# Two graph layers on one core: the last block's values laid out by tokens, its weighted sums formed by quarters

## The chip, the core and the metric

The kernel runs on one core of a Trainium2 chip. The core has five engines that work side by side and wait for each other by semaphores: TensorE (PE in the profile, its weight loads PEld), VectorE (DVE), ScalarE (ACT), GpSimd (POOL) and SyncE (SP), which here only issues transfers. The metric is the time of one execution on the device, in microseconds, as the median of several.

## What is computed

The input x is 128 graphs of 64 nodes with 768 features, adj a 64 by 64 adjacency for each graph. Layer 0 (attention by the product of x with itself, three weight matrices, a normalisation, relu) gives a residual that is added to x and normalised. Layer 1 is attention with 12 heads of 64 features over the same graphs. Its end is what this change is about:

```python
q = _split_heads(input_graph @ Wq + bq)
k = _split_heads(input_graph @ Wk + bk)
v = _split_heads(input_graph @ Wv + bv)
scores = jnp.einsum('bhqd,bhkd->bhqk', q, k) / sqrt(HD)
scores = scores + beta * adj_e                      # masked where adj is 0
probs = jax.nn.softmax(scores, axis=-1)
out = jnp.einsum('bhqk,bhkd->bhqd', probs, v)
...
x = _layernorm(x + out, axis=-1)
```

All of it is in float32.

## The kernel before

**Blocks and tiles.** The 8192 tokens are taken in 16 blocks (`NBLK`) of 512 tokens, which is 8 graphs. A block has four tiles of 128 tokens (`T`), two graphs on the partitions of a tile. A loop over n works on block n's layer 1 and block n + 1's layer 0 at once. What remains of the block before (p = n - 1) is pushed into it too.

**The order of the work** is written out by hand. A weight product of a block is computed by seven products of half-size matrices (`seven`, with the order `ORDER` = 1, 2, 6, 5, 7, 4, 3). Each of the seven has two parts j, so that there are 14 units, places 0 to 13. Each unit is three matrix calls of 128 by 128 by 384, which the profile shows as six records. Before a unit, `hooks` for its place are called. They put other work into PE's order. After a unit, `step()` takes the next pieces from three queues of prepared functions: `first`, `urgent` and `lazy`. Their tags (`act`, `root`, `after`, `gap`, `tiny`, `free`) say when a piece may be taken. `settle(key)` runs the queues until all pieces of that key are issued, and `freed()` empties `first`. The order of issue on an engine is the order in which it works.

**Values.** `values(n)` forms v with `by_tokens("v", ...)` through `seven`. A first product is evicted from PSUM with its bias into `u` (L415), and a later one, added to that, into `v`. For m and h as the halves of tokens and columns, the second product finishes (0, 0), the seventh (1, 1), the fourth (1, 0) and the third (0, 1). In all blocks but the last, v is evicted as one instruction of 128x384 (L774) and is then rearranged by three ACT copies (L786, L787). In the last block (`in_place`) each eviction is four instructions of 64x192 (L779), which write v into the rearranged places straight away.

**Scores.** `scores(n, hg)` works on one of three head groups (hg = 0, 1, 2) of four heads each. PE forms the scores, DVE multiplies by the mask (L839), adds (L860), takes the maximum (L861) and subtracts it (L862). ACT takes 16 exponentials of 32x256, each from one set of 32 partitions to another (L853), and DVE turns 32 by 32 squares in place (L857). The result is `eT`, exponentials with the key node on the partitions.

**Weighted sums.** `weighted(n, hg, halves)` multiplies `eT` with v and a column of ones, so that the sum of the exponentials comes out beside the sums. It does this for a head group and for a half of the tokens, with calls of 64 by 64 by 65. `added` takes the reciprocal of the sums (L888) and then adds the product to the residual tile in four scaled additions of 128x64 (L892).

**The last normalisation.** `finish_by_act` takes the sums (L937) and the squares (L940) of a tile on ACT, then the factors on DVE (L912, L915, L921, L922) with a root on ACT (L918), normalises on ACT (L926) and stores through POOL's queue (L930). `finish` takes DVE's statistics (L353, L354), a root on ACT (L361), normalises on DVE (L950) and stores through SP's queue (L951).

**The last block's end** was so ordered:

```python
values(n, {0: [partial(finish_by_act, n - 1, queue=lazy)], 4: [partial(scores, n, 2, 2, l0t)],
           12: [partial(weighted, n, 0, (1,))], 13: [partial(weighted, n, 1, (1,))]}, True)
...
weighted(n, 2, (1,))
settle(("y", n, 2))
finish_by_act(n, range(2, 4))
```

After these, the three head groups of the first half of the tokens follow, then `finish` for tiles 0 and 1. Scores of the third head group stand ahead of unit 4. Two of the six half groups of weighted sums are formed ahead of units 12 and 13, four after the last unit.

Of the kernel before, what the change touches and what calls it, by code (L numbers as in the profile page):

```python
# [51 lines left out]
def gnn_two_layers(ctx: ExitStack, tc, x, adj, wl, bl, ws, bs, wr, br, gamma, beta,  # L52
# [68 lines left out]
    def later(key, *fs, queue=lazy):  # L121
        queue.extend((key, f) if callable(f) else (key, *f) for f in fs)
# [635 lines left out]

        return one, two

    def values(n, hooks={}, in_place=False):

        def pairs(a):
            return a.rearrange("p (j r d) -> p r j d", r=2, d=HD)

        def last(t, h, ps, part):  # L770
            add = pairs(bias["v"][:, h * HALF : (h + 1) * HALF] if part is None else part)
            heads = slice(h * 3, (h + 1) * 3)
            if not in_place:
                nc.vector.tensor_tensor(v[:, t, :, heads, 0:HD], pairs(ps), add, ALU.add)  # L774
                return
            for r in range(2):
                for g in range(2):
                    rows = slice(g * L, (g + 1) * L)
                    nc.vector.tensor_tensor(v[r * L : (r + 1) * L, t, g, heads, 0:HD],  # L779
                                            pairs(ps)[rows, r], add[rows, r], ALU.add)  # L780

        by_tokens("v", blocks[n]["S"], last, None, hooks)
        if not in_place:
            low, high = v[0:L, :, 1, :, 0:HD], v[L:P, :, 0, :, 0:HD]
            swap = l0t.tile([P, T, HP, HD], F32, tag="lr", name="swap")
            later(("v", n), act(lambda: nc.scalar.copy(swap[0:L], high)), act(lambda: nc.scalar.copy(high, low)),  # L786
                  act(lambda: nc.scalar.copy(low, swap[0:L])), queue=urgent)  # L787
# [29 lines left out]
    def scores(n, hg, at_once=1, pool=None, gaps=1):  # L817

        blk = blocks[n]
        q, k = blk["qk"]
        settle("e")
# [21 lines left out]
        def exponentials(groups):  # L845
            if 0 in groups:
                blk["eT", hg] = (pool or l1e_p).tile([P, T, 2, P], F32, tag="lr" if pool else "eT", name="eT")
            e = blk["eT", hg].rearrange("p t c i -> p (t c) i")
            for a in groups:
                rows = slice(a * Q, (a + 1) * Q)  # L850
                for b in range(P // Q):
                    cols = slice(b * Q, (b + 1) * Q)
                    nc.scalar.activation(e[cols, :, rows], pairs[rows, :, cols], AF.Exp)  # L853

        def turn(h):
            e = blk["eT", hg][:, h * 2 : h * 2 + 2].rearrange("p t c i -> p (t c i)")
# [6 lines left out]
              *[act(partial(exponentials, range(a, a + at_once))) for a in range(0, P // Q, at_once)], *[GAP] * gaps,  # L863
              *([partial(turn, 0), partial(turn, 1)] if pool is None else [lambda: (turn(0), turn(1))]), queue=urgent)

    def weighted(n, hg, halves=range(2), heads=range(2)):


        blk = blocks[n]
        settle(("v", n))  # L870
        settle(("e", n, hg))
        freed()
        xt, eT = blk["x"], blk["eT", hg]
        y = {(r, h): ps_mm.tile([P, 2, 2, HD + 1], F32, tag="mm", name=f"ps_y{r}") for h in halves for r in range(2)}
        for h in halves:
            for t in range(2):
                for c in heads:
                    for r in range(2):
                        rows = slice(r * L, (r + 1) * L)
                        for g in range(2):  # L880
                            cols = slice(g * L, (g + 1) * L)
                            nc.tensor.matmul(y[r, h][cols, t, c, :], lhsT=eT[rows, 2 * h + t, c, cols],  # L882
                                             rhs=v[rows, 2 * h + t, g, hg + c * HC, :], start=True, stop=True)

        def added(h, r):
            ps = y[r, h][:, :, heads[0] : heads[-1] + 1, :]
            rz = st.tile([P, 2, 2], F32, tag="rz1", name="rz1")[:, :, 0 : len(heads)]
            nc.vector.reciprocal(rz, ps[:, :, :, HD])  # L888
            for t in range(2):
                res = xt[2 * h + t].rearrange("p (c k r d) -> p r c k d", c=2, k=HC, r=2)  # L890
                for k, c in enumerate(heads):
                    nc.vector.scalar_tensor_tensor(res[:, r, c, hg, :], ps[:, t, k, 0:HD], rz[:, t, k : k + 1],  # L892
                                                   res[:, r, c, hg, :], ALU.mult, ALU.add)

        later(("y", n, hg), *[partial(added, h, r) for h in halves for r in range(2)], queue=first)

    def finish_by_act(n, tiles=range(T), queue=urgent):

        xt, key = blocks[n]["x"], ("f", n)
        total, nm, var, std, rstd, shift = (st.tile([P, T], F32, tag=f"f{k}", name=f"f{k}") for k in range(6))  # L900
        some = slice(tiles[0], tiles[-1] + 1)

        def sums(fs):
            if queue is lazy:
                unused = l0t.tile([P, 2, D], F32, tag="lr", name="unused")[:, 0, :]
            else:
                unused = l1s_p.tile([P, T * 4 * L], F32, tag="s", name="unused")[:, 0:D]
            for t in tiles:
                fs(t, unused)

        def mean():
            nc.vector.tensor_scalar(nm[:, some], total[:, some], -1.0 / D, None, ALU.mult)  # L912

        def variance():
            nc.vector.tensor_scalar(std[:, some], var[:, some], 1.0 / D, 1e-5, ALU.mult, ALU.add)  # L915

        def root():
            nc.scalar.activation(std[:, some], std[:, some], AF.Sqrt)  # L918

        def factors():  # L920
            nc.vector.reciprocal(rstd[:, some], std[:, some])  # L921
            nc.vector.tensor_tensor(shift[:, some], nm[:, some], rstd[:, some], ALU.mult)  # L922

        def norm(ts):
            for t in ts:
                nc.scalar.activation(xt[t], xt[t], AF.Identity, bias=shift[:, t : t + 1], scale=rstd[:, t : t + 1])  # L926

        def stored(ts):
            for t in ts:
                nc.gpsimd.dma_start(out=out_t[n, t], in_=xt[t])  # L930

        def act(f):
            return f, "act" if queue is urgent else "root"

        settle(("y", n, 0))
        settle(("y", n, 1))
        later(key, (partial(sums, lambda t, o: nc.scalar.activation(o, xt[t], AF.Identity,  # L937
                                                                    accum_out=total[:, t : t + 1])), "after"),
              GAP, GAP, tiny(mean),
              act(partial(sums, lambda t, o: nc.scalar.activation(o, xt[t], AF.Square, bias=nm[:, t : t + 1],  # L940
                                                                  accum_out=var[:, t : t + 1]))),
              GAP, GAP, tiny(variance), act(root), GAP, tiny(factors),
              *[act(partial(norm, tiles[k : k + 2])) for k in range(0, len(tiles), 2)],
              (partial(stored, tiles[0:2]), "free"), GAP, GAP, (partial(stored, tiles[2:]), "free"), queue=queue)

    def finish(n, tiles=range(T)):
        xt = blocks[n]["x"]

        def norm(t, mean, rstd):
            nc.vector.tensor_scalar(xt[t], xt[t], mean, rstd, ALU.subtract, ALU.mult)  # L950
            nc.sync.dma_start(out=out_t[n, t], in_=xt[t])  # L951

        for t, mr in zip(tiles, moments(("f", n), [xt[t] for t in tiles], 1e-5, urgent)):
            later(("f", n), partial(norm, t, *mr), queue=urgent)

# [66 lines left out]
    for n in range(NBLK):  # L1024
# [20 lines left out]
        if p >= 0:  # L1045
            one = left if not last else qk[0]
            at(one, 2, scores, p, 2, *((1,) if last else (2, None, 4)))
            at(one, 5, weighted, p, 1)
            if not last and m < DEEP:
                at(left, 13, weighted, p, 2)  # L1050
                at(right, 0, finish_by_act, p)
            elif not last:
                at(right, 1, weighted, p, 2)
                at(right, 2, finish_by_act, p)
            else:
                at(qk[1], 5, weighted, p, 2)

# [92 lines left out]
        for hg in range(NHG):  # L1150
            projected(n, hg, qk[hg])

    n = NBLK - 1
    values(n, {0: [partial(finish_by_act, n - 1, queue=lazy)], 4: [partial(scores, n, 2, 2, l0t)],
               12: [partial(weighted, n, 0, (1,))], 13: [partial(weighted, n, 1, (1,))]}, True)
    settle(("f", n - 1))
    settle(("y", n, 0))
    settle(("y", n, 1))
    weighted(n, 2, (1,))
    settle(("y", n, 2))  # L1160
    finish_by_act(n, range(2, 4))
    step()
    for hg in range(NHG):
        weighted(n, hg, (0,))
        settle(("y", n, hg))
        step()
        step()
    finish(n, range(2))
    settle(("f", n))


# [29 lines left out]
```

## Time and profile before

| | |
|---|---|
| Median of three runs | 2934.7 us (2934.53 to 2936.67) |
| The profiled execution's own time | 2938.14 us |
| Span in its profile, first to last instruction | 2936.4 us |
| Mean granted TensorE clock | 0.995 |
| Busy: PE, DVE, ACT, POOL | 98%, 68%, 38%, 25% of the span |
| Values of the last block, PE's first unit | from 2881.7 us |
| PE's last unit ends | 2914.6 us |
| Last store issued by SP | 2932.3 us |

Times inside the execution count from its first instruction. A row of a timeline is its start, its duration, the engine, the line in the kernel, the operation, output and inputs by the names of the program, shapes and the number of instructions merged; in brackets, how long the engine had been idle and who ended that. A row of a group ends in total busy time, the mean of one in ns, and idle time before them. In the chain of waits each row is a start, a duration, and the instruction or wait that the end of the program hung on at that time.

### The profile page before, as it was taken

How to read it: one execution, taken by the hardware profiler on the slowest of the kernel's cores; microseconds unless marked ns; L12 is line 12 of the kernel's file. 1: busy time of each engine (PE TensorE's matmuls, PEld its weight loads, DVE VectorE, ACT ScalarE, POOL GpSimd, SP SyncE). 2: the span in 40 equal slices, each digit the busy share in tenths (PEclk: the TensorE clock that was granted, in tenths of full speed). 3: DMA queues.
4: the chain of work that ended last, by engine and by line, in shares of the span. 5: the costliest groups of instructions: out<-in, count | busy, mean ns of one | idle time of the engine just before them, and what ended most of it. 6: DMA issues, size and time to landing. Idle time of an engine off the chain costs nothing.

```text
span 2936.4 us, 49944 instructions
## 1 busy us (share of the span) xinstructions
PE 2879.9 (98%) x17578; PEld 1935.1 (66%) x17578; DVE 1989.5 (68%) x4034; ACT 1123.6 (38%) x2114; POOL 729.9 (25%) x879
## 2 busy tenths in 40 slices
PE   8999999999999999999999999999999999999997
PEld 5657567585665856658576575766757567585685
DVE  5678677676676766667667576666767667676656
ACT  0004324354243543434444344443434424354254
POOL 3133122304132130411405124051230413313110
PEclk9999999999999999999999999999999999999998
DMA  9788786849578595775958759486694966849442
GB/s 322 221 274 276 234 233 194 249 138 290 154 197 248 144 285 152 214 231 163 271 147 239 203 175 271 135 260 183 185 260 137 282 163 198 244 139 287 140 127 90
DMA packets 440278, 613.18 MB, mean 209 GB/s; under 512 B 53584, under 2 KB 416720, under 8 KB 440032
## 3 DMA queue, kind: packets, MB, share of 16 engines
q1 hardware_dynamic: 362096, 493.57, 56.0%
q10 hardware_dynamic: 60848, 44.05, 8.2%
q0 software_dynamic: 17088, 72.37, 6.7%
q8 instruction: 143, 2.34, 0.3%
q14 instruction: 103, 0.84, 0.1%
HBM read 539.43 MB, written 77.27 MB: 210 GB/s over the span
## 4 chain that ended last, share of the span: by engine, by line
PE 91%; ACT 3%; POOL 2%; DVE 2%; DMA 1%; issue 1%; SPq 0%; ACTq 0%; DVEq 0%
PE ps_X L384 35%; PE ps_Y L384 26%; PE ps_Y L638 11%; PE ps_X L638 10%; PE ps_ctx L677 3%; ACT eT L853 2%; PE sc L835 2%; PE ps_y L882 2%; PE u L527 2%; POOL q L337 1%; ACT L853 1%; ACT uqk L804 1%; POOL q L336 0%; PE ps_x L286 0%; DVE o L892 0%
## 5 line engine op out<-in xcount | busy, mean ns | idle before, releaser
L384 PE MATMUL ps_X<-xT,wqk 128*128 128x256 f32 x1728 | 395.9, 381 | 9.6 <-ACT uqk L804 9.6
L853 ACT ACTIVATE eT<-s 32x256 f32<-32x256 f32 x768 | 317.8, 414 | 184.7 <-DVE s L862 174.6
L384 PEld LDWEIGHTS ps_X<-xT,wqk 128*128 128x128 f32 x1728 | 325.8, 190 | 67.1 <-ACT uqk L804 16.2
L317 POOL TENSOR_TENSOR S<-hT 128x768 f32<-128x768 f32 x16 | 28.9, 1808 | 1133.4 <-PE ps_Y L384 1102.2
L384 PE MATMUL ps_Y<-S,wqk 128*128 128x256 f32 x1152 | 264.3, 379 | 0.0
L682 ACT ACTIVATE unused<-o 128x768 f32<-128x768 f32 x60 | 50.6, 843 | 500.4 <-DVE o L679 304.9
L384 PEld LDWEIGHTS ps_Y<-S,wqk 128*128 128x128 f32 x1152 | 218.9, 190 | 29.8
L438 DVE TENSOR_TENSOR lr<-ps_Y,u_deep 128x384 f32<-128x384 f32 x273 | 152.1, 557 | 108.6 <-PE ps_Y L638 82.8
L638 PE MATMUL ps_Y<-wlr,q 128*128 128x384 f32 x546 | 208.6, 491 | 0.0
L384 PE MATMUL ps_X<-wv,xT 128*128 128x384 f32 x576 | 195.0, 489 | 0.0
L804 ACT ACTIVATE uqk<-ps_X,bq 128x256 f32<-128x256 f32 x144 | 68.3, 474 | 324.9 <-PE ps_X L384 323.7
L812 DVE TENSOR_TENSOR q<-ps_Y,uqk 128x256 f32<-128x256 f32 x144 | 61.0, 424 | 177.7 <-ACT uqk L804 89.4
L384 PE MATMUL ps_X<-ws,hT 128*128 128x384 f32 x540 | 179.4, 486 | 0.1
L892 DVE SCALAR_TENSOR_TENSOR o<-ps_y,rz,o 128x64 f32<-128x64 f32 x768 | 165.0, 277 | 6.8
L638 PE MATMUL ps_X<-wlr,q 128*128 128x384 f32 x364 | 151.1, 497 | 14.5 <-POOL q L337 5.9
L384 PEld LDWEIGHTS ps_X<-wv,xT 128*128 128x128 f32 x576 | 108.2, 190 | 80.8 <-issue 8.4
L438 DVE TENSOR_TENSOR u_deep<-ps_X,lr 128x384 f32<-128x384 f32 x195 | 107.3, 550 | 68.0 <-PE ps_X L638 66.4
L384 PEld LDWEIGHTS ps_X<-ws,hT 128*128 128x128 f32 x540 | 102.4, 190 | 71.8 <-DMA ws<-in_L_gnn_W_self_dram 0.7
L638 PEld LDWEIGHTS ps_Y<-wlr,q 128*128 128x128 f32 x546 | 101.6, 190 | 67.2
L415 DVE TENSOR_TENSOR u<-ps_X,bv 128x384 f32<-128x384 f32 x96 | 53.4, 556 | 130.3 <-PE ps_X L384 130.2
L384 PE MATMUL ps_X<-S,wqk 128*128 128x256 f32 x576 | 138.2, 385 | 0.0
L384 PE MATMUL ps_Y<-xT,wqk 128*128 128x256 f32 x576 | 135.6, 385 | 0.0
(247 smaller groups left out, 5482.6 us busy)
## 6 DMA issues: line engine op xcount, KB each, us to landing
wlr<-lr_d SPq DMA_DIRECT2D x819, 192.0 KB, 3.5
wqk<-qk_d SPq DMA_DIRECT2D x672, 192.0 KB, 2.4
wv<-d_v SPq DMA_DIRECT2D x192, 192.0 KB, 3.3
ws<-d_s SPq DMA_DIRECT2D x180, 192.0 KB, 6.0
wv<-in_L_gnn_Wv_dram SPq DMA_DIRECT2D x144, 192.0 KB, 4.1
ws<-in_L_gnn_W_self_dram SPq DMA_DIRECT2D x135, 192.0 KB, 5.5
xa<-in_x_dram SPq DMA_DIRECT2D x64, 384.0 KB, 5.4
out_dram<-o POOLq DMA_DIRECT2D x62, 384.0 KB, 6.2
```

Source lines behind the costliest of these rows:

```text
L384: nc.tensor.matmul(ps, lhsT=a, rhs=b, start=(c == 0 and i in (1, 2, 5)), stop=(c == len(fs) - 1), skip_group_check=True)
L415: recent["u"] = evicted[nm] = nc.vector.tensor_tensor(u, ps, bias[nm][:, b * HALF : (b + 1) * HALF], ALU.add)
L438: nc.vector.tensor_tensor(dst, view(ps), add, ALU.add)
L527: nc.tensor.matmul(u[g * L : (g + 1) * L, t, :], lhsT=xT[:, c, tok], rhs=xT[:, c, tok], start=(c == 0), stop=(c == KC - 1))
L638: nc.tensor.matmul(ps, lhsT=a, rhs=b, start=(k == 0 and j in (1, 2, 5)), stop=(k == len(fs) - 1), skip_group_check=True)
L677: nc.tensor.matmul(ps[g * L : (g + 1) * L, 0:HALF], lhsT=blk["aT"][:, t, g * L : (g + 1) * L], rhs=blk["lr"][t][:, g, cols], start=True, s ...
L804: nc.scalar.activation(u, ps, AF.Identity, bias=bias["qk"[j]][:, c : c + 1])
L812: nc.vector.tensor_tensor(dst, ps, part, ALU.add)
L835: nc.tensor.matmul(sc[r][g * L : (g + 1) * L, t, c, :], lhsT=q[rows, c, tok], rhs=k[rows, c, tok], start=True, stop=True)
L853: nc.scalar.activation(e[cols, :, rows], pairs[rows, :, cols], AF.Exp)
L882: nc.tensor.matmul(y[r, h][cols, t, c, :], lhsT=eT[rows, 2 * h + t, c, cols], rhs=v[rows, 2 * h + t, g, hg + c * HC, :], start=True, stop= ...
L892: nc.vector.scalar_tensor_tensor(res[:, r, c, hg, :], ps[:, t, k, 0:HD], rz[:, t, k : k + 1], res[:, r, c, hg, :], ALU.mult, ALU.add)
```

## The change

Only the last block changes. Its order on each engine is the same as before up to the values of the last block.

- `values` evicts v by tokens in the last block too, one instruction of 128x384 in place of four of 64x192. With `stay` there is no rearranging afterwards.
- The exponentials of the last block go to other partitions and columns of `eT`, so that the key node of graph g stands on g's 64 partitions: 16 instructions of the same size as before.
- Weighted sums are formed by `quarter(h, c)`: half of the tokens (h) by half of the columns (c), for all three head groups, 24 calls of 64 by 64 by 65 each. For each r (two heads interleaved) one reciprocal of 128x6 and one product of 128x384 from PSUM write the quotient into `shares`. Then `added` adds a 128x384 piece of `shares` to each of two residual tiles, on POOL or on DVE.
- Three quarters stand ahead of units 10, 11 and 13, one behind the last unit. Scores of the third head group move from place 4 to place 2.
- All four tiles take DVE's statistics, half a tile at a time; tiles 3, 2 and 1 are normalised by ACT and stored through ACT's queue, tile 0 by DVE and stored through SP's.
- For block n - 1, `finish` with `queue=lazy` puts the squares of its tiles on ACT ahead of the third group's exponentials, and its four stores go through SP's queue, not POOL's.

The core of the diff:

```diff
-            if not in_place:
-                nc.vector.tensor_tensor(v[:, t, :, heads, 0:HD], pairs(ps), add, ALU.add)
-                return
-            for r in range(2):
-                for g in range(2):
-                    rows = slice(g * L, (g + 1) * L)
-                    nc.vector.tensor_tensor(v[r * L : (r + 1) * L, t, g, heads, 0:HD],
-                                            pairs(ps)[rows, r], add[rows, r], ALU.add)
+            nc.vector.tensor_tensor(v[:, t, :, heads, 0:HD], pairs(ps), add, ALU.add)
...
-                    nc.scalar.activation(e[cols, :, rows], pairs[rows, :, cols], AF.Exp)
+                    to = (b, a) if n < NBLK - 1 else (a // 2 * 2 + b % 2, b // 2 * 2 + a % 2)
+                    to = [slice(k * Q, (k + 1) * Q) for k in to]
+                    nc.scalar.activation(e[to[0], :, to[1]], pairs[rows, :, cols], AF.Exp)
...
+            begin = (summed, "after"), GAP, (lambda: (mean(), squared()), "act"), GAP, GAP, tiny(variance), act(root),                 GAP, GAP, GAP, tiny(factors)
...
+    def quarter(h, c):
+        for hg in range(NHG):
+            settle(("e", n, hg))
+        freed()
+        y = [ps_mm.tile([P, 2, NHG, HD + 1], F32, tag="mm", name=f"ps_y{r}") for r in range(2)]
+        for r in range(2):
+            for k in range(NHG):
+                for t in range(2):
+                    for g in range(2):
+                        rows = slice(g * L, (g + 1) * L)
+                        nc.tensor.matmul(y[r][rows, t, k, :], lhsT=blk_e[k][rows, 2 * h + t, c, r * L : (r + 1) * L],
+                                         rhs=v[rows, 2 * h + t, r, c * HC + k, :], start=True, stop=True)
...
+        def divided(r):
+            rz = small[:, 2 * h : 2 * h + 2, 32 + 8 * c + 4 * r : 32 + 8 * c + 4 * r + NHG]
+            nc.vector.reciprocal(rz, y[r][:, :, :, HD])
+            nc.vector.tensor_tensor(by_head[:, :, r], y[r][:, :, :, 0:HD],
+                                    rz[:, :, :, None].to_broadcast([P, 2, NHG, HD]), ALU.mult)
+
+        def added(t, engine):
+            res = xt[2 * h + t][:, c * HALF : (c + 1) * HALF]
+            engine.tensor_tensor(res, res, share[:, t, :], ALU.add)
...
+    def behind(h, c):
...
+        later(("q", h, c), partial(divided, 0), lambda: (divided(1), added(0, nc.gpsimd), added(1, nc.gpsimd)),
+              queue=first)
...
+    def norm_by_act(t):
+        nc.scalar.activation(xt[t], xt[t], AF.Identity, bias=shift[:, t], scale=rstd[:, t])
+        nc.scalar.dma_start(out=out_t[n, t], in_=xt[t])
...
+    def before_last():
+        divided, added = quarter(1, 0)
+        for t in (2, 3):
+            measured(t, 1)
+        divided(0)
+        divided(1)
+        added(0, nc.gpsimd)
+        added(1, nc.vector)
...
+    values(n, {0: [partial(finish, n - 1, queue=lazy)], 2: [partial(scores, n, 2, 2, l0t)],
+               10: [partial(behind, 0, 0)], 11: [partial(behind, 1, 1)],
+               12: [freed, partial(measured, 0, 0), partial(measured, 1, 0)], 13: [before_last]}, True)
     settle(("f", n - 1))
...
+    divided, added = quarter(0, 1)
+    for t in (3, 2):
+        measured(t, 0)
+        whole(t)
+    factors(slice(2, 4))
+    divided(0)
+    inverse(slice(2, 4))
+    for t in (3, 2):
+        norm_by_act(t)
+    divided(1)
+    added(1, nc.gpsimd)
+    added(0, nc.vector)
+    for t in (0, 1):
+        measured(t, 1)
+        whole(t)
+    factors(slice(0, 2))
+    inverse(slice(0, 2))
+    nc.vector.tensor_scalar(xt[0], xt[0], mv[:, 0, 0:1], rstd[:, 0], ALU.subtract, ALU.mult)
+    nc.sync.dma_start(out=out_t[n, 0], in_=xt[0])
+    norm_by_act(1)
```

Here `measured(t, c)` takes the statistics of half a tile, `whole(t)` aggregates the two halves, `factors` adds epsilon (DVE) and takes the root (ACT), and `inverse` forms the factors on DVE.

## The prediction

> **What bounds the kernel now.** The page comes first. TensorE is busy for 98% of the span, and only its last slices fall off; the diff touches nothing but the last block's values and what follows them. So the question is one of the last 55 us, and I cut these into stretches.
>
> ```profile
> PE 2879.9 (98%) x17578; PEld 1935.1 (66%) x17578; DVE 1989.5 (68%) x4034; ACT 1123.6 (38%) x2114; POOL 729.9 (25%) x879
> ...
> 2881.00:2900.00 19.00, 19.00 (x122) 11.64 (x121) 11.80 (x22) 6.45 (x16) 0.00 (x0) 1.00 0.15 44
> 2900.00:2912.00 12.00, 10.54 (x71) 5.93 (x73) 8.40 (x22) 10.08 (x21) 0.00 (x0) 1.00 0.01 1
> 2912.00:2920.00 8.00, 4.63 (x99) 3.14 (x93) 7.68 (x35) 1.80 (x2) 0.00 (x0) 0.94 0.00 0
> 2920.00:2928.00 8.00, 3.35 (x77) 2.82 (x71) 7.26 (x41) 6.00 (x12) 2.17 (x4) 0.50 0.52 196
> ```
>
> The last four rows are the windows view: length, then busy time of PE, PEld, DVE, ACT and POOL, then the clock granted to TensorE. Up to 2900 PE has no gap; from 2912 DVE has none (7.68 of 8.00) and PE works half the time. The chain of waits says the same: it leaves PE at 2900.6 and is DVE's nearly alone to the end.
>
> ```profile
> 2900.63 0.57 DVE u L415
> 2901.23 0.35 DVE v L779
> ...
> 2911.88 0.35 DVE v L779
> ...
> 2920.25 0.86 DVE o L892 x4
> ...
> 2931.05 0.68 DVE o L950
> ```
>
> DVE's timeline gives the size of each piece: an eviction of values is four instructions and 1.46 us; a group of weighted sums is a reciprocal and four scaled additions, 0.98 us from one to the next. From ACT's and SP's timelines I take the exponentials of the third head group and the last two stores.
>
> ```profile
> 2911.88 1.46 DVE L779 TENSOR_TENSOR v<-ps_Y,u 64x192 f32<-64x192 f32 x4 [2.46 <-PE ps_Y L384]
> 2919.07 0.17 DVE L888 RECIPROCAL rz<-ps_y 128x4 f32<-128x4 f32 x1
> 2919.27 0.86 DVE L892 SCALAR_TENSOR_TENSOR o<-ps_y,rz,o 128x64 f32<-128x64 f32 x4
> 2920.05 0.17 DVE L888 RECIPROCAL rz<-ps_y 128x4 f32<-128x4 f32 x1
> 2897.81 6.82 ACT L853 ACTIVATE eT<-s 32x256 f32<-32x256 f32 x16 [12.37 <-DVE s L862]
> 2931.76 0.93 SPq L951 DMA_DIRECT2D out_dram<-o  x2
> ```
>
> The second store issues at 2932.34 and lands at about 2935.17 (2.83 us); the closing barrier takes 1.23 us more, to 2936.40. That tail I carry over.
>
> **Values by tokens.** An eviction becomes one 128x384 instruction. Other blocks have it:
>
> ```profile
> L774 DVE TENSOR_TENSOR v<-ps_Y,u 128x384 f32<-128x384 f32 x90 | 50.1, 557 | 67.7 <-PE ps_Y L384 66.7
> L452 POOL TENSOR_TENSOR lr<-lr,bias_lr 128x384 f32<-128x384 f32 x52 | 52.1, 1001 | 4.1 <-DVE rz L888 4.1
> L234 DVE TENSOR_TENSOR t_r<-b_r,t_r 128x384 f32<-128x384 f32 x6 | 3.1, 551 | 0.1
> L353 DVE BATCH_NORM_STATS2 stats<-o 128x6 f32<-128x384 f32 x140 | 69.3, 537 | 0.1
> ```
>
> 0.56 for 1.46 is 0.90 us less, eight times. Two of the eight lie under PE's full stretch and bring nothing; six lie after 2901, 5.4 us less on DVE's path.
>
> **Scores two units earlier.** PE's units of six records last 1.94 us (3.87 for two in the chain). From 2881.73 two units end at 2885.6, the scores (1.09) at 2886.7. DVE then runs the mask product, addition, maximum and subtraction (rows 1.29, 1.21, 1.21, 1.22) between evictions, to 2894.6. On ACT the squares of block 14 (4.2) now stand ahead of the exponentials; the mean they need comes at 2890.8, so they run to 2895.1 and the exponentials to 2901.9 (6.82); turns (1.31) end at 2903.2, not 2907.7. PE reaches place 10 at 2902.4 and the first quarter's third head group waits 0.6 us for the turns. Behind that wait in PE's order stand four units and three quarters; DVE waits for them.
>
> **Quarters instead of groups.** PE: 96 calls before and after, two records each. A block of 64 records takes 1.09, so a quarter of 48 takes 0.82. But successive calls now use only two of the four (row half, column half) places, which no 64-by-64 call here shows. If that halves the rate a quarter takes 1.6, and my sum grows by 1.0. The calls that form u alternate between two column halves and start four records in 0.058 us, as the 64-by-64 calls do in 0.059, so I take 0.82. At the clock of 0.50 in the last stretch 32 records took 1.46, so 48 would take 2.2; for the last quarter that ends its halves at 2916.9 and 2918.0, ahead of their use at 2917.4 and 2918.4, and costs nothing. PE's last unit then ends at 2913.2, where it ended at 2914.6.
>
> DVE: twelve groups at 0.98, 11.8 us, become eight halves of a quarter: reciprocal 0.18, gap 0.04, product of 384 out of PSUM 0.56, less 0.08 overlap, 0.70 each, 5.6 us. Eight additions of 128x384 appear: six on POOL at 1.00, two on DVE at 0.55. The statistics of tiles 2 and 3, sums and squares on ACT before (four passes, 4.1 us with their reads), become four more statistics (0.54) and two aggregates (0.21) on DVE: 2.6 more. One of two closing 0.68 normalisations moves to ACT (1.02), beside the other.
>
> **DVE's path, step by step.** The fourth unit from the end ends at 2905.75; its eviction at 2906.5, quarter one divided at 2908.2 (with 0.36 for block 14's factors). Next eviction (PE 2908.5) 2909.25, quarter two 2910.6. POOL adds quarter one 2908.25 to 2910.25 and quarter two 2910.7 to 2912.7. Two statistics, an eviction, a statistic: 2912.5; a wait of 0.3 for POOL, statistic, 2913.35. Quarter three 2914.7, DVE's addition 2915.3, last eviction 2915.8. PE's last quarter 2915.8 to 2916.6. Meanwhile two statistics with aggregates, the second behind POOL's addition, 2917.3; epsilon, first half divided 2918.15, factors 2918.45. ACT normalises tiles 3 and 2 and issues each store (0.36, as ACT's loads): done 2921.2, before its next root at 2921.9. DVE: second half 2919.1, addition 2919.7, statistic and aggregate 2920.55; POOL's addition to 2920.8; statistic and aggregate 2921.7; epsilon, root, reciprocal, shift 2922.5. DVE ends tile 0 at 2923.1, ACT tile 1 at 2923.6 and issues at 2923.62. Against 2932.34 that is 8.7 us earlier.
>
> Block 14's four stores leave POOL for SP, at 0.34 an issue: SP's last load went at 2885.5 and its next store is due at 2923, so this costs nothing; on POOL they would hold up the additions.
>
> **POOL and DVE together** is the price with two ends. Twice an addition on DVE and one on POOL are released by the same product. Rows of the trace:
>
> ```profile
> 502.63 1.21 DVE L862 TENSOR_TENSOR s<-s,mx 128x1024 f32<-128x1024 f32 x1
> 502.64 1.51 POOL L337 TENSOR_TENSOR q<-q,S 128x128 f32<-128x128 f32 x1
> ...
> 563.00 1.85 POOL L323 TENSOR_TENSOR S<-S,xT 128x768 f32<-128x768 f32 x1
> 563.22 1.91 DVE L757 TENSOR_TENSOR add<-add,off 128x256 f32<-128x256 f32 x1
> ```
>
> Whoever starts first makes the other wait: POOL's 0.46 became 1.51, DVE's 0.43 became 1.91. DVE follows its own product after 0.04, POOL after 0.08 to 0.15, so I take DVE first, as in the path. POOL first would put DVE's additions 1.0 and 0.8 later: 1.8 in all. Statistics and evictions beside POOL (0.55, 0.56) show no stretching.
>
> The Trainium skill speaks against the six additions on POOL: "GPSIMD Engine Reference", section Engine selection, gives elementwise additions to VectorE, GpSimd being about twice as slow on two inputs. The rows agree on the ratio (1.00 to 0.55). All eight additions on DVE would put 6 x 0.47 = 2.8 on its path and take two waits of 0.3 off it, so the sum by the rule would be 2.1 worse than mine with POOL.
>
> **Sum.** The profiled execution took 2938.14 us, 1.74 over its span and 3.4 over the median of 2934.7, so I carry the difference: 2934.7 - 8.7 = 2926.0. Own range 2925 to 2928: better by about 1 if the store lands as SP's first of the pair (2.4) and waits shrink; worse by 1.8 if POOL is first.
>
> **Rivals.**
> - Contention and PE both at their dear ends: 8.7 - 1.8 - 1.0 = 5.9 saved, 2928.8. The 0.04 against 0.08 speaks against the first, u's calls against the second. Chance 0.12.
> - The last store through ACT's queue lands late. ACT's loads land after 6.9 and 8.1 us in the median, in full traffic; their least is 2.9, and at the end only two or three stores are under way. At 6.9 the gain is 8.7 - 4.1 = 4.6: 2930.1. Chance 0.11.
> - Slower: PE, in order, stands at place 10 before the third head group's turns. Each microsecond that these end after 2903.2 delays everything by one; from 2911.9 the gain is gone. It would take, say, two further rounds like the 16 exponentials (13.6) on ACT: 8.7 - 13.6, 4.9 slower, 2939.6. Against it: in this trace scores to turns took 17.0 us with DVE late; from 2886.7 that is 2903.7. Chance 0.04.
> - The cuts do not add up because DVE waits for PE or POOL wherever it became shorter: PE's units alone end only 1.4 earlier, and with that gain the time is 2933.3. Speaks against it that 17.7 us of DVE work followed PE's last unit. Chance 0.03.
>
> **How the numbers follow.** About 0.2% (5.9 us, to 2928.8) is what a measurement here can tell from no change. The forecast has 0.70; faster takes 0.08 of the first rival: 0.78. Within: 0.04 + 0.11 + 0.03 = 0.18. Slower 0.04. The range 2924.5 to 2930.5 holds the first three cases.
>
> **What would show it.** After: evictions of 0.56 in the last values; turns of the third group by 2903.5; under 1 us of PE waiting before the first quarter; DVE's work after PE's last unit 10.4 us, not 17.7; the two paired additions at 0.55 on DVE and 1.5 on POOL; span near 2927.7. Wrong if turns end after 2906, if DVE's paired additions last 1.5, or if the last landing takes over 4.

## The result and the profile after

The changed kernel takes 2929.75 us in the median (2927.76 to 2932.23, 20 runs), the kernel before beside it 2936.64 (20 runs): a ratio of 0.9977 [0.9971, 0.9984], 6.9 us less. The forecast of 2926.0 was 3.7 too low. Its sign was right, and its wide range, 2924.5 to 2930.5, holds the result; its own range of 2925 to 2928 does not.

Up to the last values both programs issue the same order, yet the profile of after comes to PE's first unit there 1.8 us earlier (2879.92 for 2881.73). In the fourteen profiles of this document that unit starts anywhere between 2876.8 and 2882.1, so the difference says nothing of the change. So I compare stages from that unit, and cut them at the issue of the last store: the *path* lies before it, the *closing* behind it (landing, then the barrier of all engines).

| us, from the profiles | PE's last unit ends | path | closing | stage |
|---|---|---|---|---|
| before | 32.87 | 50.62 | 4.08 | 54.70 |
| forecast | 31.5 | 41.9 | 4.06 | 46.0 |
| after | 33.77 | 42.77 | 6.96 | 49.73 |

The path is 7.85 shorter, where 8.7 was forecast. The closing is 2.9 longer, where nothing was.

The page of after, first part, and then its windows (length, busy PE, PEld, DVE, ACT, POOL, granted clock, DMA share, GB/s):

```profile
PE 2875.0 (98%) x17578; PEld 1932.9 (66%) x17578; DVE 1979.8 (68%) x3973; ACT 1120.5 (38%) x2107; POOL 732.1 (25%) x879
```

```profile
2900.00:2912.00 12.00, 12.00 (x167) 8.17 (x166) 8.11 (x20) 5.21 (x6) 3.77 (x4) 1.00 0.35 133
2912.00:2920.00 8.00, 3.45 (x54) 2.23 (x52) 7.36 (x22) 1.89 (x3) 2.88 (x3) 0.90 0.04 15
2920.00:2930.00 10.00, 0.00 (x0) 0.00 (x0) 1.76 (x6) 1.60 (x3) 0.00 (x0) 0.50 0.38 147
```

PE now has no gap until 2912 (12.00 of 12.00, where it had 10.54), and 61 of DVE's instructions are gone. In the last stretch PE and POOL do nothing, and DVE and ACT 1.76 and 1.60 us of ten: something else ends the program.

PE's timeline of after shows two of the quarters, the units between them, and the last quarter:

```profile
2904.33 1.62 PE L1164 MATMUL ps_y<-v,eT 64*64 64x65 f32 x48
...
2909.94 1.62 PE L1164 MATMUL ps_y<-v,eT 64*64 64x65 f32 x48
2911.49 2.20 PE L384 MATMUL ps_Y<-wv,S 128*128 128x384 f32 x6
...
2915.24 1.50 PE L1164 MATMUL ps_y<-v,eT 64*64 64x65 f32 x44 [1.28 <-DVE v L772]
```

A quarter of 48 records takes 1.62 us by these rows and 1.54 to 1.55 from its start to the next row's, not 0.82. DVE's and POOL's timelines show the cheap eviction and the last quarter's pair of additions:

```profile
2908.12 0.56 DVE L772 TENSOR_TENSOR v<-ps_X,bv 128x384 f32<-128x384 f32 x1 [1.45 <-PE ps_X L384]
...
2917.87 0.56 DVE L1174 TENSOR_TENSOR shares<-ps_y,small 128x384 f32<-128x384 f32 x1
2918.46 0.56 DVE L1179 TENSOR_TENSOR o<-o,shares 128x384 f32<-128x384 f32 x1
```

```profile
2910.20 1.95 POOL L1179 TENSOR_TENSOR o<-o,shares 128x384 f32<-128x384 f32 x2 [1.43 <-PE ps_Y L384]
2914.20 1.37 POOL L1179 TENSOR_TENSOR o<-o,shares 128x384 f32<-128x384 f32 x1 [2.05 <-DVE shares L1174]
2918.50 1.36 POOL L1179 TENSOR_TENSOR o<-o,shares 128x384 f32<-128x384 f32 x1 [2.93 <-DVE shares L1174]
```

DVE starts its addition 0.04 us ahead of POOL and keeps 0.56; POOL's 1.00 becomes 1.36. The chain of waits of after, its end:

```profile
2914.20 1.37 POOL o L1179
2915.57 2.90 issue
2918.47 1.41 POOLq L1272
...
2921.63 1.03 ACT o L1206
```

It ends at ACT's normalisation; the store issues at 2922.69 and lands at 2925.51. SP is ready for the barrier at 2925.65, yet the span ends at 2929.7. The row to look at is POOLq L1272, the program's closing: it is POOL's DRAIN record, called its drain here. The chain cuts this drain short where DVE goes on; the trace's own record of it, which no row of the views shows at its full length, runs from 2918.47 to 2928.87, 9.00 us past the end of POOL's last addition (2919.87). Before, POOL's closing drain ended at 2933.81, ahead of the last landing, and cost nothing.

### The profile page after: what moved, and what is told of

It is laid out like the page before. It is cut to its first block, busy times and chain, and to the rows that moved or that the text cites. A ratio compares the mean times of both kernels' runs of the same rounds, so it can differ in the third digit from the quotient of the medians.

```text
span 2929.7 us, 49874 instructions
## 1 busy us (share of the span) xinstructions
PE 2875.0 (98%) x17578; PEld 1932.9 (66%) x17578; DVE 1979.8 (68%) x3973; ACT 1120.5 (38%) x2107; POOL 732.1 (25%) x879
## 4 chain that ended last, share of the span: by engine, by line
PE 92%; ACT 3%; POOL 2%; DMA 1%; DVE 1%; issue 1%; POOLq 0%; SPq 0%; ACTq 0%; DVEq 0%
PE ps_X L384 36%; PE ps_Y L384 26%; PE ps_Y L638 11%; PE ps_X L638 10%; PE ps_ctx L677 3%; ACT eT L848 2%; PE sc L828 2%; PE ps_y L877 2%; PE u L527 2%; POOL q L337 1%; ACT L848 1%; ACT uqk L796 1%; POOL q L336 0%; DMA b_r<-in_L_gnn_W_right_dram 0%; PE ps_x L286 0%
## 5 line engine op out<-in xcount | busy, mean ns | idle before, releaser
L887 DVE SCALAR_TENSOR_TENSOR o<-ps_y,rz,o 128x64 f32<-128x64 f32 x720 | 154.7, 278 | 6.4
```

## The experiments

What POOL's drain hangs on had three candidates: always 9 us after its last tensor instruction; the stores, which now go out through ACT's queue; or the absence of transfers issued by POOL shortly before. The other experiments price the terms of the sum. Paths, closings and stages are each read from one profile, medians and ratios from all executions of a run.

**The change again, and its last POOL addition on VectorE.**

> The changed kernel once more, as the yardstick for the runs beside it. Both theories: the path from PE's first unit of the last values to the issue of the last store 42.8 us (50.6 before), the closing from that issue to the end 6.9 us (4.1 before), GpSimd's drain ending about 9.0 us after its last addition. If the closing's length only came with that one execution, it will be near 4.1 here and the span about 3 shorter.

Measured: 2929.62 us against 2936.41 before, ratio 0.9977 [0.9968, 0.9987]. Its stage is 49.74, with the drain again 9.00 past POOL's last instruction: the 6.96 is no accident of one execution.

```diff
-    added(1, nc.gpsimd)
     added(0, nc.vector)
+    added(1, nc.vector)
```

> Only the last quarter's addition of tile 1 goes from GpSimd to VectorE, so GpSimd's last instruction ends about 4.3 us earlier (at about 2915.6 on the clock of the profile after). Theory A (GpSimd's drain takes some 9 us from its last tensor instruction, and the program's end waits for it): drain ends near 2924.6, before the last store lands; closing back to 4.1, path 42.8 to 43.1 (the two additions now follow each other on VectorE, 0.5, for 0.4 of waiting and blocking), so the kernel is about 2.7 us faster than the change as it stands. Theory B (the closing is long because the last store goes through ACT's queue, or the drain ends some 3.3 us after the last landing whatever GpSimd did): closing stays 6.9, no gain.

Measured: 2927.40 us, 0.9969 [0.9957, 0.9980]; path 42.88, closing 3.79, stage 46.66, 3.1 less than the change as it stands. The median is 2.2 below that of the change beside it (2929.62), with overlapping intervals; the argument rests on the closing. The end of its chain of waits no longer holds a row of POOL's:

```profile
2919.49 1.03 DVE o L1179 x2
2920.52 0.48 DVE small L1192
...
2922.78 1.03 ACT o L1206
```

POOL's last instruction ends at 2916.61 and the drain at 2925.61: 9.00 again, but now ahead of the last landing. The stores still go through ACT's queue, so these are not the cause.

**All eight additions on VectorE** (every `added(…, nc.gpsimd)` becomes `nc.vector`).

> All six additions of GpSimd go to VectorE. Path: by the sum 1.2 longer than the change as it stands (six additions of 0.48 on VectorE less its waits for GpSimd), 44.0. Theory A: GpSimd's last tensor instruction is 90 us away, closing 4.1, so 1.6 us faster than the change as it stands and about 1.2 slower than the run with one addition moved. Theory B: closing 6.9, 1.2 slower than the change as it stands. The published rule for the engines (additions on VectorE) would have the path no longer.

Measured: 2928.22 us, 0.9968 [0.9956, 0.9981]; path 44.04, closing 3.74, stage 47.78. POOL's last instruction is then of the block before (2825.11), and its drain ends 9.00 later, some 90 us before the end.

**One late POOL addition on the kernel before.** Both versions add a sum whose result nothing uses; everything else is the kernel before.

```diff
+    spare = [l0t.tile([P, 2, D], F32, tag="lr", name="spare")[:, 0, 0:HALF] for _ in range(1)][0]
+    nc.gpsimd.tensor_tensor(spare, bias["v"][:, 0:HALF], affine_of["beta"][:, 0:HALF], ALU.add)
```

> The kernel before with one more GpSimd addition of 128x384 on unused tiles, placed behind its last two stores (its result is used by nothing). VectorE's and ACT's work is untouched. Theory A: GpSimd ends the addition near 2932.0, its drain some 9 us later, so the closing grows from 4.1 to about 9.5 and the kernel is about 5 us slower than before. Theory B: the addition ends before the last landing, closing 4.1, no difference.

Measured: 2936.49 us, 0.9999 [0.9990, 1.0008]. The addition ran at 2920.40, ahead of POOL's two stores of that kernel, so the question stayed open. In the second version it reads a tile that DVE writes last, and stands behind the stores:

```diff
+    spare = l0t.tile([P, 2, D], F32, tag="lr", name="spare")[:, 0, 0:HALF]
+    nc.gpsimd.tensor_tensor(spare, blocks[n]["x"][1][:, 0:HALF], affine_of["beta"][:, 0:HALF], ALU.add)
```

> The kernel before with one GpSimd addition of 128x384 more, which reads the normalised tile 1 and writes a tile that nothing uses, so that it can only start when VectorE has ended the kernel's work (some 50.7 us after PE's first unit of the last values). Theory A (9.0 us from GpSimd's last tensor instruction to the end of its drain, whatever follows): addition 1.0, drain 9.0, closing part 0.75 more: from the last store's issue to the end some 10.8 us for 4.1, 6.7 us slower than before. Theory B (the drain follows the stores): the addition ends before the last landing, 4.1 stays.

Measured: 2936.59 us, 1.0001 [0.9992, 1.0011], closing 4.09. The addition ended at 2933.69 and the drain at 2934.85, after 1.16 and not 9. "Always 9" falls. POOL had issued two stores just before (2929.73 and 2930.65).

**The same late addition, with no store on POOL's queue.** The second version of above, and:

```diff
-                nc.gpsimd.dma_start(out=out_t[n, t], in_=xt[t])
+                (nc.sync if n >= NBLK - 2 else nc.gpsimd).dma_start(out=out_t[n, t], in_=xt[t])
```

> The kernel before with the late GpSimd addition (which ended in a drain of 1.2 us), and now with the stores of block 14 and of tiles 2 and 3 on SP's queue, so that GpSimd issues no transfer in the last 100 us. Path 50.6, or 51.8 to 52.3 where TensorE's clock halves in unit 12 as in the two other runs of this order. Theory C: drain 9.0 after the addition, closing 10.8, about 6 us slower than before. If it is not the transfers that matter (place of the addition, or its operands): closing 4.1.

Measured: 2942.12 us, 1.0021 [1.0012, 1.0030]: slower than before. Path 50.62, as before; closing 10.82. The chain of waits of this run ends with POOL's closing row, which the chain cuts off some 10 us ahead of the span's end:

```profile
core 0 of [0], span 2938.8 us
...
2927.98 1.03 POOLq L1199
```

POOL's addition ends at 2929.01, the drain at 2938.01. With and without POOL's stores the same late addition is followed by 1.16 or 9.00.

**The reverse, on the changed kernel:** block 14's four stores go through POOL's queue again.

```diff
-                (nc.sync if ends else nc.gpsimd).dma_start(out=out_t[n, t], in_=xt[t])
+                nc.gpsimd.dma_start(out=out_t[n, t], in_=xt[t])
```

> The change with block 14's four stores back on GpSimd's queue; they fall between its fifth and its last addition. Path 42.8 in both cases. Theory A as first put (9.0 us from GpSimd's last tensor instruction to the end of its drain, always): closing 6.96 again, though the late addition in the kernel before had 1.2. Theory C (the 9.0 us come only when GpSimd has issued no transfer shortly before its end; with one, the drain ends with the transfers' landing or about 1.2 us after the last instruction): the drain ends by about 44 us after PE's first unit, closing 4.1 or less, 2.9 us faster than the change as it stands.

Measured: 2928.35 us, 0.9972 [0.9962, 0.9983]. POOL's timeline:

```profile
2915.60 2.16 POOL L925 DMA_DIRECT2D out_dram<-o  x4 [1.61 <-ACT small L1199]
2917.78 1.01 POOL L1179 TENSOR_TENSOR o<-o,shares 128x384 f32<-128x384 f32 x1
```

The drain ends 4.18 after the addition (2918.78 to 2922.97) and no longer decides. The path is 43.26, 0.5 longer, because POOL's last addition stands behind the stores and DVE waits 0.8 us for POOL where it waited 0.3. The last store lands after 3.87, for 2.82, so that the closing misses the expected 4.1; it was issued at 2921.60, while block 14's last store was still on its way (to 2922.46). The closing is 5.01, the stage 48.27. So the transfers shorten the drain here too: with these stores left on POOL's queue the closing is 1.95 shorter than in the change. The drain ends 0.51 us after POOL's last store lands. In the kernel before it ends 0.59 after that landing (2933.22 to 2933.81), in the first version with an added sum 0.58 (2929.53 to 2930.11). So where POOL stored shortly before, its drain ends soon after the landing.

**The price of a quarter.** The first run forms half of each quarter's sums only: tiles 1 and 3 get those of tiles 0 and 2, and PE makes 12 calls for 24.

```diff
-                for t in range(2):
+                for t in range(1):
...
```

The lines left out let VectorE read the one tile's sums twice.

> The change, but each quarter's 24 calls become 12: only the first of its two tiles is multiplied, and VectorE reads that one's sums for both (so tiles 1 and 3 get those of 0 and 2). VectorE's instructions keep their sizes. Theory: the quarter's calls at 0.0325 us a record, twice the rate assumed, put the term of 1.0 on the path; at half the calls PE's last unit of the values ends 2.1 us earlier (31.7 after the first, for 33.8) and the path is 41.5, 1.3 less than 42.8. Rival: VectorE's own work sets the path, and PE's time is hidden: 42.8 stays.

Measured (one run): 2927.14 us; path 41.37, PE's last unit at 31.68. PE's timeline:

```profile
2897.83 0.92 PE L1164 MATMUL ps_y<-v,eT 64*64 64x65 f32 x24
```

So with quarters near the forecast's 0.82 (0.85 from start to start) PE's last unit ends near the forecast's 31.5, and the path is half a microsecond better than forecast. The second run forms all the sums, but stays at one 64-by-64 place of the array for six calls (twelve records), where the change alternates between two:

```diff
-            for k in range(NHG):
-                for t in range(2):
-                    for g in range(2):
+            for g in range(2):
+                for k in range(NHG):
+                    for t in range(2):
```

> The change with the loop over g outside: six calls in a row (twelve records) use the same quarter of the array, where successive calls alternated between two. Theory: a quarter of the array takes a 64-by-64-by-65 record every 0.065 us, so that 64 records on four places took 1.09 and 48 on two take 1.55; on one place 48 take about 3.1, PE's last unit ends 4 us or more later and the path is longer by 3 us or more. Rival: the calls are limited elsewhere (issue, weights, the write to PSUM) and the order of places does not matter: 1.55 and 42.8.

Measured (one run): 2935.2 us; path 44.48, 1.7 longer. PE's timeline:

```profile
2902.78 2.47 PE L1164 MATMUL ps_y<-v,eT 64*64 64x65 f32 x48
```

A quarter takes 2.47, and 2.40 from its start to the next unit's at 2905.18, where 3.1 was expected. A record costs 0.050 us at one place after the other, 0.032 in the change's order (1.54 for 48 in its chain), and 0.017 in the kernel before (1.09 for 64). From two places to one only the order changed, so the number of places in turn matters, though one place is not twice as dear as two. From four to two the change also altered which PSUM tile successive calls write, and no run separates the two.

**The scores back at place 4.**

```diff
-    values(n, {0: [partial(finish, n - 1, queue=lazy)], 2: [partial(scores, n, 2, 2, l0t)],
+    values(n, {0: [partial(finish, n - 1, queue=lazy)], 4: [partial(scores, n, 2, 2, l0t)],
```

> The change with the third head group's scores at place 4, as before, the rest as it is. By my sum the turns end 2.8 us later, the first quarter waits for them on PE, and everything behind it is 2.8 later: path 45.6, closing 6.9; so the move of the scores is worth 2.8 us. Rival: the wait falls into time that VectorE or PE lose anyway: path under 44.

Measured: 2933.65 us, 0.9993 [0.9984, 1.0002]; path 47.14, PE's last unit at 37.78, so 4.0 later. PE's timeline, the first quarter and the unit behind it:

```profile
2901.68 2.00 PE L1164 MATMUL ps_y<-v,eT 64*64 64x65 f32 x32 [2.27 <-DVE eT L852]
2903.61 2.88 PE L384 MATMUL ps_X<-wv,xT 128*128 128x384 f32 x6
```

PE waits 2.27 us at place 10 for the third head group's turns, as said, and then runs that unit in 2.88 for 2.20. The windows show why: from 2901.6 to 2905.0 the granted clock is 0.50. The 32 records behind the wait then take 1.93 us (about 1.0 at the change's rate) and the unit 0.7 more, which with the wait makes nearly all of the 4.0. The expectation of 2.8 had the wait, but not this loss. The move of the scores is worth 4.4 us of path.

**Four evictions again**, of 64x192, in the new layout and in the last block alone.

```diff
+            for r in range(2):
+                for g in range(2):
+                    rows = slice(g * L, (g + 1) * L)
+                    nc.vector.tensor_tensor(v[rows, t, r, heads, 0:HD], pairs(ps)[rows, r], add[rows, r], ALU.add)
```

> The change with each eviction of the last values cut into four instructions of 64x192 again, at the places the change gives them. By my sum the path is 3.1 us longer, 45.9, not the 5.4 that six evictions of 0.90 less make, since VectorE waits for PE and GpSimd in places. Rival: all six count, 48.2; or PE sets the path there, under 44.

Measured: 2934.12 us, 0.9996 [0.9987, 1.0006]; path 46.90, stage 53.86. DVE's timeline:

```profile
2903.23 1.46 DVE L778 TENSOR_TENSOR v<-ps_X,bv 64x192 f32<-64x192 f32 x4 [0.64 <-PE ps_X L384]
```

The single eviction is worth 4.1 us of path. Both moves were needed: take either of them away, leave the longer closing, and the changed kernel can't be told from the kernel before.

**The best version.** As in the first experiment the last addition is VectorE's, and DVE no longer waits 0.27 us for POOL in front of a statistic: `measured(3, 1)` stands behind the first product.

```diff
-        for t in (2, 3):
-            measured(t, 1)
+        measured(2, 1)
         divided(0)
+        measured(3, 1)
         divided(1)
```

> The run with the last addition on VectorE, and the statistic of tile 3 behind the first half of the third quarter, so that VectorE has something to do while GpSimd ends its fourth addition. The profile after shows that wait as 0.27 us. If it is on the path: path 42.6 for 42.9, closing 3.8, stage 46.4. If VectorE waits for PE later anyway: 42.9.

Measured: 2925.45 us against 2935.83, ratio 0.9964 [0.9950, 0.9977]; path 42.50, closing 3.79, stage 46.29. It is the shortest of all stages here, 3.4 below the change, and the whole is 10.4 us below the kernel before.

## Why the prediction was right, and where it was 3.7 us off

**Evictions: right.** Each takes 0.56, as put. The forecast had six of them worth 5.4; taken alone they bring 4.1, since part of what DVE saves is then spent waiting for PE (in front of the two `v<-ps_X` evictions DVE waits 3.6 us in all in the change and 1.1 with four instructions each).

**Scores two units earlier: right.** Turns ended 21.3 us after the first values unit, forecast 21.5, and PE did not wait visibly for them, where 0.6 had been put.

**A quarter at 0.82: the mis-sized term.** It takes 1.5 to 1.6, which the prediction had as its dear end, with "my sum grows by 1.0". That bound was somewhat low: against half the calls the cost is 1.4 of path (42.77 less 41.37). The calls that form u were the wrong nearest row. They have 128 rows and alternate two column halves; a 64-by-64 call that alternates two places shows half the rate of four. The last unit ended at 33.77, not 31.5.

**Divided halves, statistics and the work after PE's last unit: slightly too dear.** The forecast had 10.4 us from there to the last store; it was 9.0. In the run with half the calls, where PE's last unit ended near the forecast, it was 9.7 (31.68 to 41.37): 0.7 of the difference is these terms. The other 0.7 is likely work that DVE had already done while PE was late; no run shows that apart. With PE's last unit 2.3 later (33.77 for 31.5) and the rest 1.4 shorter, the path came out 0.9 above the forecast's 41.9.

**POOL and DVE together: right.** DVE went first both times and kept 0.56; POOL took 1.37 and 1.36 where 1.5 was said. The rival's 1.8 was not seen.

**The last store on ACT's queue: right.** It landed after 2.82, forecast 2.83; the rival with a landing of 6.9 was not seen. Nor was the slower rival: PE had its gap at place 10 only when the scores went back to place 4.

**"That tail I carry over": the step that failed.** The landing could be carried over, the closing barrier of 1.23 could not. The change takes POOL's last transfers away and gives POOL a late addition, and then POOL's drain of 9.00 us ends 3.2 us after SP is ready. That cost 2.9, three quarters of the stage's miss of 3.7 (49.73 for 46.0). The prediction followed POOL's four stores to SP's queue and priced their issue, but did not ask what POOL itself still owes when the program ends. That the wide range still held the result is luck in this respect: its upper end was drawn for a last store that lands late (2930.1), not for this. Before, POOL's drain ended 1.4 us ahead of the last landing (2933.81 to 2935.17), so that no row of the end hung on it.

**The rule on the additions.** The Trainium skill, "GPSIMD Engine Reference", section Engine selection, gives elementwise additions to VectorE. The forecast had all eight additions on DVE 2.1 dearer (its terms, 2.8 less 0.6, give 2.2). On the path it is 1.3 dearer (44.04 for 42.77), so POOL's help is real; for the whole stage it is 2.0 cheaper (47.78 for 49.73), for a reason that is not the rule's. Best is the mixture: POOL for the early additions, none in the last quarter.

**The rest of the 6.9.** The medians differ by 6.9, where 8.7 was forecast; the forecast was set against 2934.7, the three runs shown, and the kernel before has 2936.64 here. So of the 3.7 us by which the median missed, 1.9 is this base and 1.8 the saving; that the stage missed by 3.7 too is chance. In the two profiles the stage is 5.0 shorter. A part of the difference may lie in the kernel before. In the profiles of the first two versions with one addition more, whose order on PE is that of before, TensorE's clock falls to half in the last but one unit of the values. The timeline and the windows of the second of them, and the windows of before's own profile at the same place:

```profile
2906.77 1.77 PE L882 MATMUL ps_y<-v,eT 64*64 64x65 f32 x16 [1.28 <-DVE v L779]
2908.46 3.68 PE L384 MATMUL ps_Y<-wv,S 128*128 128x384 f32 x6
```

```profile
2905.00:2908.00 3.00, 1.53 (x27) 0.98 (x28) 2.82 (x7) 2.92 (x7) 0.00 (x0) 1.00 0.02 5
2908.00:2911.00 3.00, 3.00 (x14) 1.85 (x15) 0.08 (x1) 1.03 (x2) 0.00 (x0) 0.51 0.00 0
```

```profile
2910.00:2912.00 2.00, 2.00 (x19) 0.99 (x21) 0.12 (x1) 0.36 (x2) 0.00 (x0) 1.00 0.00 0
```

The unit takes 3.68 at a clock of 0.51, and 2.20 in the profile of before at 1.00. Before it PE was idle for 1.28 us in one piece, waiting for an eviction, and for 1.47 of the 3.00 us from 2905 to 2908. Of four profiles with this order two fell (stages of 55.9 and 56.4), two did not (the kernel before with 54.7, and the version with all stores on SP's queue). In the changed kernel PE has no such idle ahead of its last unit, which ends at 33.77 in the profiles of the change, of its repeat, of the three runs that move additions or a statistic to other places and of the one with block 14's stores on POOL. So the change also takes away a loss that the one profile of before did not show: against executions such as these two it saves 6.2 to 6.6. How often the kernel before falls into it was not counted. The interval of the medians reaches down to 4.7 us; the remaining difference is within it.

The Trainium skill, "TensorE: Matmul & The Clock Gate", section What's actually happening, has the clock go to half after an idle window of about 3.4 us whose position runs freely. A fall in some executions and not in others, with nearly the same idle, fits the free position, and in both the trace's record of the clock has it at half for 3.41 us. But PE was not idle for a whole such stretch (1.47 of 3.00 us); where the two differ, the measurement decides.

## What to carry to other kernels

When a change moves an engine's last work, look at what that engine does between its last instruction and the end of the program, also where it costs nothing today; in this kernel GpSimd's drain ended 9.00 us after its last tensor instruction wherever it had issued no transfer shortly before, and where that came last the barrier waited for it. Price a burst of small matrix calls by a row with the same number of array places in turn, and not by size alone. A gain can hang on two moves at once: here nothing measurable was left of it when either the cheap eviction or the earlier scores was taken away.

## What the runs showed of the hardware

- GpSimd's closing drain ends 9.00 us after its last tensor instruction when POOL issues no transfer near the end, in all ten such profiles. With transfers issued by POOL shortly before that instruction it ended 1.16 us (version of the kernel before) and 4.18 us (version of the changed kernel) behind it, and where the landing of POOL's last store came later than its last tensor instruction, 0.51 to 0.59 us behind that landing (three profiles). What POOL does in those 9 us, and how a transfer cuts it short, stays open.
- Calls of 64 by 64 by 65 cost 0.017, 0.032 and 0.050 us a record with four places in turn, two places in turn, and one place at a time; from four to two the order over PSUM tiles changed too.
- TensorE's clock fell to half in two of four executions of the same order, after PE had been idle for 1.28 us in one piece (1.40 and 1.47 of 3.00 us in all), and in the run with the scores at place 4 after a wait of 2.27 us. Each fall lasted 3.41 us.
